# Router logits from the graphs' first rows on the vector engine, and expert choice on all partitions

## The chip, the cores and the metric

The kernel runs on one core of one Trainium2 chip. The metric is the device time of one execution in microseconds (us). Before the change it is 1921.93 us, the median of three runs (1921.78 to 1924.34).

## The reference

128 graphs of 128 nodes, each node with 1024 features, go through two blocks, each added to its input. `adj` has ones at about 3% of its places.

```python
def reference(x, adj, L0_gnn_W, L0_gnn_a, L0_ffn_router_w, L0_ffn_lora_down, L0_ffn_lora_up):
    x = x + gnn(layernorm(x), adj, W, a)
    x = x + ffn(layernorm(x), router_w, lora_down, lora_up)
    return x

def gnn(h, adj, W, a):                      # 16 heads of 64 features
    Wh = (h @ W) split into heads
    e = leaky_relu(Wh @ a[:, :, :F] + Wh @ a[:, :, F:], 0.2)
    att = softmax(where(adj == 0, -9e15, e)) * adj
    return elu(att @ Wh)

def ffn(x, router_w, lora_down, lora_up):   # 8 experts of rank 16, 2 chosen per graph
    logits = einsum('bh,eh->be', x[:, 0, :], router_w)
    gates = softmax over the 2 largest logits, 0 elsewhere
    down = einsum('blh,erh->bler', x, lora_down)
    return x + einsum('bler,ehr,be->blh', down, lora_up, gates)
```

So the router looks only at the first row (node 0) of each graph, and chooses two experts for the whole graph.

## The kernel before, in words

**Tiling.** The kernel works in passes over pairs of graphs (q = 0 to 63, then two more passes that finish the last group). Four graphs make a group g, so a group has an even pass and an odd one. Activations stand with the 128 nodes on the partitions; for products over the features it also has transposed copies. The matrix product with W is done per pair by seven products of blocks instead of eight (`project`, a Strassen-like scheme): each is eight fp32 products of 128x128 by 260 columns, which the profile records as 16. They are named by what they read: xt, or the sums s that GpSimd forms in `pair_sums`. A bank is a two-bank PSUM tile; three names x, y, z share two slots, so a product can start only when DVE or ACT has read the bank that it takes. Product 7 and product 4 share one accumulation, with a DVE read (L426) after each.

**Order.** The engines' order is written out by hand: the loop at the end of the kernel builds eight lists of tasks, `gaps[0]` to `gaps[7]`, runs the tasks of one list, then one of the seven products (in the order 1, 6, 2, 5, 7, 3, 4), then the next list. The order in which the tasks are called is the order on each engine, and each engine works strictly in this order. SP and ACT issue most transfers; on them a transfer that waits for something holds up all that stands behind it.

**One pair.** Pass q projects pair q, and in the same pass the pair before it (graphs i and i+1) is attended (`attend`, ph, L535), updated (`update`: hp L545, exp on ACT, xn L553 and L554) and measured (`second_stats`). `turn` then splits xn into 16-bit halves on ACT (L585) and transposes it by DMA (tt, L587), `rejoin` (y_t, L591) puts the halves together on ACT, and `join` (L607) forms y in place. `high` (L487, ACT) and `low` (L491, DVE) write the projected values in two parts for the next `attend`. Blocks 0 and 1 of the parts belong to the pair's first graph, 2 and 3 to its second.

**The feed-forward block of group g.** In the even pass (q = 2g + 2), in gap 6 between product 3 and product 4, `logits` multiplies column 0 of each graph's y_t by the router on PE: eight products of 4-column weights, with 8 moving columns (L615, 16 records), and one that brings the four graphs' rstd of row 0 onto four partitions (L618). `choose` takes on DVE the two largest logits of each graph, on 4 partitions: a `max` of eight values and then the position of each. In front of the last product of the same pass ACT computes exp of the difference (`ratio`). In the odd pass, gap 0, `fetch` spreads the chosen experts to all partitions by one product (pb, L683), forms row addresses on DVE (L686 to L693), and GpSimd gathers the experts' rows (eight transfers for down, L696, and one for up, L700). `weigh` forms the two gates on 4 partitions, and SP writes them to device memory and reads them back, one per partition (L654, L661). `ffn_down` (pd, L710, gap 4) needs the gathered rows and y_t; `ffn_up` (pu, L726) and DVE (L730) finish the group, and SP stores it.

**The last group** can't hide its gathers, so it multiplies with all experts (`down_dense`, `gates_dense`, `up_dense`), with expert tables loaded into W's place. `gates_dense` brings the gates onto the partitions by one more product (pg, L772).

**Once.** `experts` (L286) takes the mean out of the router and of the down tables, with partial sums on PE (`table_parts`, L280), and writes the down table to device memory for the gathers.

The functions and the lines of the order that matter here:

Of the kernel before, what the change touches and what calls it, by code (L numbers as in the profile page):

```python
# [8 lines left out]
F32 = mybir.dt.float32  # L9
F32R = mybir.dt.float32r  # L10
I32 = mybir.dt.int32
U32 = mybir.dt.uint32
# [13 lines left out]
def adj_ffn_kernel(  # L26
# [9 lines left out]
    a_t: bass.AP,  # L36
    down_t: bass.AP,
# [6 lines left out]
    P = 128  # L44
# [5 lines left out]
    E = router_t.shape[2]  # L50
# [7 lines left out]
    NG, _, G, _ = adj.shape  # L58
    QC = HALF // 2
# [20 lines left out]
    table = dram.tile([E * P, KC * R], F32, name="table")  # L80

# [54 lines left out]
    router_sb = const.tile([P, KC, E], F32, name="router_sb")  # L136
    down_sb = work.tile([P, G * TOP, R, KC], F32, tag="down", name="down_sb", bufs=1)

    def load_experts():
        nc.sync.dma_start(router_sb, router_t)  # L140
        nc.sync.dma_start(down_sb, down_t)
# [14 lines left out]
    ones_r = const.tile([P, P], F32R, name="ones_r")  # L156
    nc.vector.tensor_scalar(ones_r, mean_of, float(D), None, op0=ALU.mult)
    spread = const.tile([P, G, TOP], F32R, name="spread")
    nc.vector.memset(spread.bitcast(F32), 0.0)

    order = const.tile([G, E], F32, name="order")
    for e in range(E):
        nc.vector.memset(order[:, e:e + 1], float(E - e))

# [115 lines left out]
    def table_parts():  # L280
        return fourths([router_sb[:, k] for k in range(KC)],
                       [down_sb.rearrange("p e r k -> p k (e r)")[:, k] for k in range(KC)])

    slot = down_row = up_row = None

    def experts(part):  # L286

        nonlocal slot, down_row, up_row
        pr = ps_m.tile([P, HALF], F32, tag="pm", name="pr")
        nc.tensor.matmul(pr[:, 0:E + ER], sum_of, part, start=True, stop=True)  # L290
        for t, lo, n in ((router_sb.rearrange("p k e -> p e k"), 0, E),
                         (down_sb.rearrange("p e r k -> p (e r) k"), E, ER)):
            nc.vector.tensor_tensor(t, t, pr[:, lo:lo + n, None].to_broadcast([P, n, KC]),
                                    ALU.subtract)
        nc.sync.dma_start(table.rearrange("(e p) c -> p e c", p=P),
                          down_sb.rearrange("p e r k -> p e (r k)"))

        slot = const.tile([P, G * TOP], F32, name="slot")
        nc.vector.tensor_reduce(slot, ident.rearrange("p (j r) -> p j r", r=R), AX.X, ALU.add)
# [195 lines left out]
    def attention_weights(q):  # L495
# [8 lines left out]
        e = small.tile(shape, F32, tag="e", name="e")  # L504
# [6 lines left out]
        m = small.tile(shape, F32, tag="m", name="m")  # L511
        nc.vector.tensor_tensor(m, e, neg, ALU.max)
        p = small.tile([P, 2, 2, H], F32, tag="p", name="p")
# [4 lines left out]
        z = small.tile([P, 2, 2, H], F32, tag="z", name="z")  # L518
        nc.vector.tensor_mul(z, p, st["n"][:, :, pair, None].to_broadcast(z.shape))
        den = small.tile(shape, F32, tag="den", name="den")  # L520
# [88 lines left out]

    def logits(g):  # L610

        st = GRP[g]
        pl = ps_m.tile([P, HALF], F32, tag="pm", name="pl")
        for k in range(KC):
            nc.tensor.matmul(pl[:G, 0:E], st["y_t"][:, k, 0:G * P:P], router_sb[:, k],  # L615
                             start=(k == 0), stop=(k == KC - 1))

        nc.tensor.matmul(pl[:G, E:E + 1], st["rstd"], ident[:, 0:1], start=True, stop=True)  # L618
        st["pl"] = pl

    def choose(g):

        st = GRP[g]
        both = small.tile([G, E + 1], F32, tag="lg", name="lg")
        nc.vector.tensor_copy(both, st["pl"][:G, 0:E + 1])
        lg, dev = both[:, 0:E], both[:, E:E + 1]
        top = small.tile([G, 8], F32, tag="top", name="top")
        nc.vector.max(out=top, in_=lg)

        val = small.tile([G, 2, TOP], F32, tag="val", name="val")  # L630
        first = small.tile([G, E], F32, tag="first", name="first")
        mark = small.tile([G, 2, E], F32, tag="mark", name="mark")
        for s in range(TOP):
            nc.vector.scalar_tensor_tensor(mark[:, s], lg, top[:, s:s + 1], order,
                                           op0=ALU.is_equal, op1=ALU.mult)
            if s:
                nc.vector.tensor_scalar(first, order, val[:, 0, 0:1], None, op0=ALU.is_equal)
                nc.vector.scalar_tensor_tensor(mark[:, s], first, float(-E), mark[:, s],
                                               op0=ALU.mult, op1=ALU.add)
            nc.vector.tensor_reduce(val[:, 0, s:s + 1], mark[:, s], AX.X, ALU.max)  # L640
        if g < NG - 1:

            nc.vector.tensor_tensor(spread[0:G], ident[:G, :G, None].to_broadcast([G, G, TOP]),
                                    val[:, None, 0].to_broadcast([G, G, TOP]), ALU.mult)
        pr = small.tile([G, 2], F32, tag="pr", name="pr")
        nc.vector.tensor_sub(pr[:, 0:1], top[:, 1:2], top[:, 0:1])
        st.update(val=val, pr=pr, dev=dev)

    def put_away(val, name):

        own = small.tile([G, TOP, R], F32, tag="own", name="own", bufs=2)
        nc.vector.tensor_copy(own, val[:, :, None].to_broadcast([G, TOP, R]))
        rows = dram.tile([P, 1], F32, tag=name, name=name, bufs=2)
        nc.sync.dma_start(rows.rearrange("(g r) o -> g (r o)", g=G),  # L654
                          own.rearrange("g s r -> g (s r)"))
        return rows

    def of_rows(rows, name):

        mine = small.tile([P, 1], F32, tag=name, name=name)  # L660
        nc.sync.dma_start(mine, rows)  # L661
        return mine

    def ratio(g):
        st = GRP[g]
        nc.scalar.activation(st["pr"][:, 1:2], st["pr"][:, 0:1], AF.Exp, scale=st["dev"])

    def weigh(g):

        st = GRP[g]  # L670
        gate, pr = st["val"][:, 1], st["pr"]
        nc.vector.tensor_scalar(gate[:, 0:1], pr[:, 1:2], 1.0, None, op0=ALU.add)
        nc.vector.reciprocal(gate[:, 0:1], gate[:, 0:1])
        nc.vector.tensor_mul(gate[:, 1:2], pr[:, 1:2], gate[:, 0:1])
        if g < NG - 1:
            st["gate"] = of_rows(put_away(gate, "gates"), "gate")

    def fetch(g):

        st = GRP[g]  # L680
        pb = ps_m.tile([P, HALF], F32, tag="pm", name="pb")
        every = pb[:, 0:G * TOP]
        nc.tensor.matmul(every, ones_r, spread.rearrange("p g s -> p (g s)"), start=True,  # L683
                         stop=True)
        own = small.tile([P, G * TOP], F32, tag="own_slot", name="own_slot", bufs=1)
        nc.vector.tensor_tensor(own, every, slot, ALU.mult)  # L686
        mine = small.tile([P, 1], F32, tag="of_slot", name="of_slot", bufs=1)
        nc.vector.tensor_reduce(mine, own, AX.X, ALU.add)
        at_down = small.tile([P, G * TOP], U32, tag="at_down", name="at_down")
        nc.vector.tensor_scalar(at_down, every, float(-P), down_row, op0=ALU.mult,  # L690
                                op1=ALU.add)
        at_up = small.tile([P, 1], U32, tag="at_up", name="at_up")
        nc.vector.tensor_scalar(at_up, mine, float(-R), up_row, op0=ALU.mult, op1=ALU.add)  # L693
# [46 lines left out]
    down_all = block[1][:, 0:D].rearrange("p (k e r) -> p k e r", e=E, r=R)  # L740

    def load_all():
        nc.sync.dma_start(down_of_rows.rearrange("p e r k -> p e (r k)"),
                          table.rearrange("(e p) c -> p e c", p=P))
        nc.sync.dma_start(up_all, up_t)

# [13 lines left out]
    def gates_dense(g):  # L760

        st = GRP[g]
        val = st["val"]
        chosen = small.tile([G, TOP, E], F32, tag="chosen", name="chosen", bufs=1)
        for s in range(TOP):
            nc.vector.tensor_scalar(chosen[:, s], order, val[:, 0, s:s + 1], val[:, 1, s:s + 1],
                                    op0=ALU.is_equal, op1=ALU.mult)
        rows = work.tile([G, E, R], F32, tag="hp", name="chosen_rows")
        nc.vector.tensor_tensor(rows, chosen[:, 0, :, None].to_broadcast([G, E, R]),
                                chosen[:, 1, :, None].to_broadcast([G, E, R]), ALU.add)  # L770
        pg = ps_m.tile([P, HALF], F32, tag="pm", name="pg")
        nc.tensor.matmul(pg[:, 0:G], rows.rearrange("g e r -> g (e r)"), ident[:G, :G],  # L772
                         start=True, stop=True)
        gate = small.tile([P, G], F32, tag="gate_all", name="gate_all", bufs=1)
        nc.vector.tensor_copy(gate, pg[:, 0:G])
# [62 lines left out]
    for q in range(NQ + 2):  # L838
# [5 lines left out]
        if ffn and not part:  # L844
            gaps[6] += [(logits, g), (choose, g)]
        if q < NQ:
            gaps[6] += [(high, q, 3), (high, q, 1)]
            gaps[7].append((high, q, 2))
# [4 lines left out]
        if 0 < q <= NQ:  # L853
# [13 lines left out]
            gaps[5] += [(join, i), (join, i + 1)]  # L867
        if q + 1 < NQ:
# [3 lines left out]
            if q:  # L872
                gaps[4].append((first_stats, 2 * q + 3))
# [82 lines left out]
```

## Time and profile before

| what | value |
|---|---|
| median of three runs | 1921.93 us |
| the profiled execution, its own time | 1922.47 us |
| its span, first to last instruction | 1920.7 us |
| TensorE (PE) busy | 1903.6 us, 99% |
| weight loads (PEld), beside PE | 1565.7 us, 82% |
| VectorE (DVE) busy | 1630.6 us, 85% |
| ScalarE (ACT) busy | 1088.3 us, 57% |
| GpSimd (POOL) busy | 832.2 us, 43% |
| mean granted TensorE clock | 0.996 |
| logits products L615 and L618 | 17.8 us and 6.0 us busy |
| pb product L683 | 11.2 us busy |

How to read it: a busy share is an average over the whole run. PE's records overlap (a weight load and the next product run under the last one), so the durations of short products add up to more than they cost; distances between starts are the safer measure. Idle time is given in brackets behind a row of the timeline, with what ended it. In the chain of work that ended last, each step goes back to what released it.

### The profile page before, as it was taken

How to read it: one execution, taken by the hardware profiler on the slowest of the kernel's cores; microseconds unless marked ns; L12 is line 12 of the kernel's file. 1: busy time of each engine (PE TensorE's matmuls, PEld its weight loads, DVE VectorE, ACT ScalarE, POOL GpSimd, SP SyncE). 2: the span in 40 equal slices, each digit the busy share in tenths (PEclk: the TensorE clock that was granted, in tenths of full speed). 3: DMA queues.
4: the chain of work that ended last, by engine and by line, in shares of the span. 5: the costliest groups of instructions: out<-in, count | busy, mean ns of one | idle time of the engine just before them, and what ended most of it. 6: DMA issues, size and time to landing. Idle time of an engine off the chain costs nothing.

```text
span 1920.7 us, 30166 instructions
## 1 busy us (share of the span) xinstructions
PE 1903.6 (99%) x11003; PEld 1565.7 (82%) x11003; DVE 1630.6 (85%) x3416; ACT 1088.3 (57%) x1060; POOL 832.2 (43%) x1135
## 2 busy tenths in 40 slices
PE   9999999999999999999999999999999999999997
PEld 6888888888888888888888888888888888888885
DVE  5888988888988888888889888888888888888886
ACT  2656556556556555565565565565565655655653
POOL 3245434355344455334454443553444553344540
PEclk9999999999999999999999999999999999999998
DMA  7565655665656656566656556556556565566562
GB/s 299 142 186 132 199 172 153 192 172 147 197 171 164 190 153 169 179 158 190 186 132 198 172 153 192 170 149 194 172 167 188 147 176 178 158 190 187 123 168 95
DMA packets 348666, 329.27 MB, mean 171 GB/s; under 512 B 279016, under 2 KB 281064, under 8 KB 348008
## 3 DMA queue, kind: packets, MB, share of 16 engines
q1 hardware_dynamic: 330792, 285.39, 50.9%
q0 software_dynamic: 17008, 40.91, 7.3%
q8 instruction: 87, 1.43, 0.3%
q10 hardware_dynamic: 720, 1.06, 0.2%
q14 instruction: 59, 0.48, 0.1%
HBM read 193.58 MB, written 67.65 MB: 136 GB/s over the span
## 4 chain that ended last, share of the span: by engine, by line
PE 91%; DVE 4%; ACT 2%; DMA 2%; issue 1%; POOL 0%; DVEq 0%; POOLq 0%; ACTq 0%
PE pw L418 77%; PE ph L535 6%; PE pu L726 3%; PE pd L710 3%; DMA tt<-halves 1%; PE pl L615 1%; ACT y_t L591 1%; DVE xn L554 1%; ACT halves L585 1%; DVE xn L553 1%; DVE hp L545 1%; DVE stats L315 1%; PE pu L787 0%; DMA down<-table,at_down 0%; PE idle L149 0%
## 5 line engine op out<-in xcount | busy, mean ns | idle before, releaser
L418 PE MATMUL pw<-w_sb,xt 128*128 128x260 f32 (+1 forms) x4080 | 939.2, 385 | 0.0
L418 PEld LDWEIGHTS pw<-w_sb,xt 128*128 128x128 f32 x4080 | 764.4, 190 | 144.9 <-issue 24.9
L418 PE MATMUL pw<-w_sb,s 128*128 128x260 f32 (+1 forms) x3072 | 709.6, 384 | 1.9 <-DVE u L426 1.9
L418 PEld LDWEIGHTS pw<-w_sb,s 128*128 128x128 f32 x3072 | 581.9, 190 | 117.4 <-POOL xt L371 22.8
L319 POOL TENSOR_SCALAR rstd<-mv 128x2 f32<-128x2 f32 x126 | 27.4, 218 | 824.8 <-DVE mv L316 819.6
L591 ACT COPY y_t<-tt 128x2048 uint16<-128x2048 uint16 x126 | 315.1, 2510 | 76.1 <-DMA tt<-halves 75.8
L696 POOL DMA_INDIRECT down<-table,at_down x248 | 251.5, 1014 | 163.4 <-DVE e L509 89.8
L585 ACT COPY halves<-xn 128x2048 uint16<-128x2048 uint16 x126 | 239.3, 1899 | 145.0 <-DVE xn L554 145.0
L315 DVE BATCH_NORM_STATS2 stats<-xn 128x6 f32<-128x512 f32 x504 | 319.0, 675 | 0.1
L487 ACT ACTIVATE parts<-wh,rstd 128x512 fp32r<-128x512 f32 x192 | 133.8, 716 | 203.8 <-DVE wh L426 203.7
L552 ACT ACTIVATE ex<-hp 128x1024 f32<-128x1024 f32 x128 | 135.3, 1057 | 189.8 <-DVE hp L545 189.8
L730 DVE SCALAR_TENSOR_TENSOR xn<-pu,rstd,xn 128x512 f32<-128x512 f32 x248 | 169.0, 745 | 21.8 <-PE pu L726 21.8
L545 DVE TENSOR_TENSOR hp<-ph,att 128x512 f32<-128x512 f32 x256 | 161.1, 670 | 10.0 <-PE ph L535 9.7
L554 DVE SCALAR_TENSOR_TENSOR xn<-ex,xn 128x1024 f32<-128x1024 f32 x128 | 156.8, 1225 | 14.3 <-DVE xn L553 0.9
L535 PE MATMUL ph<-parts,adj_f 128*128 128x512 f32 x512 | 164.4, 442 | 1.3 <-ACT parts L487 0.8
L553 DVE SCALAR_TENSOR_TENSOR xn<-hp,xn 128x1024 f32<-128x1024 f32 x128 | 156.8, 1225 | 4.4
L607 ACT ACTIVATE xn<-xn,off,mul 128x1024 f32<-128x1024 f32 x128 | 151.3, 1231 | 1.5 <-POOL off L572 1.5
L426 DVE TENSOR_TENSOR wh<-pw,u 128x520 f32<-128x520 f32 (+1 forms) x128 | 89.2, 697 | 71.6 <-PE pw L418 62.6
L491 DVE SCALAR_TENSOR_TENSOR parts<-wh,rstd,parts 128x512 fp32r<-128x512 f32 x192 | 138.0, 746 | 11.3 <-ACT parts L487 11.3
L426 DVE TENSOR_TENSOR wh<-pw,p 128x520 f32<-128x520 f32 (+1 forms) x64 | 44.8, 700 | 81.9 <-PE pw L418 81.9
L535 PEld LDWEIGHTS ph<-parts,adj_f 128*128 128x128 f32 x512 | 96.6, 189 | 20.8 <-ACT parts L487 1.2
L320 POOL TENSOR_TENSOR rstd<-rstd,half_pow 128x2 f32<-128x2 f32 x126 | 89.7, 712 | 10.5
(154 smaller groups left out, 1448.3 us busy)
## 6 DMA issues: line engine op xcount, KB each, us to landing
xn<-in_x SPq DMA_DIRECT2D x128, 512.0 KB
xt<-in_x_t SPq DMA_DIRECT2D x127, 512.0 KB
out_y<-xn SPq DMA_DIRECT2D x124, 512.0 KB
adj_f<-in_adj_t POOLq DMA_DIRECT2D x32, 256.0 KB, 3.1
adj_i<-in_adj SPq DMA_DIRECT2D x32, 256.0 KB
down<-table,at_down POOLq DMA_INDIRECT x248, 4.1
w_sb<-in_w SPq DMA_DIRECT2D x3, 1040.0 KB
wt_sb<-in_w_t SPq DMA_DIRECT2D x1, 2048.0 KB
```

The source lines that it names most:

```text
L315: nc.vector.bn_stats(st[:, h, :], X[i][:, h * HALF:(h + 1) * HALF])
L418: nc.tensor.matmul(dst[:, j, cols], lhs[:, k, :], w_sb[:, rhs, k, j, cols], start=(first and k == 0), stop=(k == KH - 1), skip_group_check ...
L491: nc.vector.scalar_tensor_tensor(in_two(PARTS[q][:, 1, b]), block, rstd, in_two(PARTS[q][:, 0, b].bitcast(F32)), op0=ALU.mult, op1=ALU.sub ...
L535: nc.tensor.matmul(PH[i][h], GRP[g]["adj_f"][:, t, :], PARTS[q][:, s, NH * (i % 2) + h], start=(s == 0), stop=(s == 1))
L545: nc.vector.tensor_tensor(hp[:, h * HALF:(h + 1) * HALF].rearrange("p (h f) -> p h f", f=F), ph.rearrange("p (h f) -> p h f", f=F), att[:, ...
L553: nc.vector.scalar_tensor_tensor(xt, hp, 0.0, xt, op0=ALU.max, op1=ALU.add)
L554: nc.vector.scalar_tensor_tensor(xt, ex, 1.0, xt, op0=ALU.min, op1=ALU.add)
L585: nc.scalar.copy(halves, X[i].bitcast(U16).rearrange("p (d s) -> p s d", s=2))
L591: nc.scalar.copy(y_of(i).bitcast(U16).rearrange("p k (n s) -> p s k n", s=2), TT.pop(i).rearrange("p (s k) n -> p s k n", s=2))
L607: nc.scalar.activation(X[i], X[i], AF.Identity, bias=GRP[g]["off"][:, t:t + 1], scale=GRP[g]["mul"][:, t:t + 1])
L696: nc.gpsimd.indirect_dma_start(out=st["down"][:, j * R:(j + 1) * R].rearrange("p r k -> p (r k)"), out_offset=None, in_=table, in_offset=b ...
L730: nc.vector.scalar_tensor_tensor(y[:, cols], pu[t], st["rstd"][:, t:t + 1], y[:, cols], op0=ALU.mult, op1=ALU.add)
```

## The change

- The router no longer stands transposed on PE's side. `router_sb` now holds 32 features of each expert per partition: partition p belongs to graph p // 32 of the group and to features 32 (p % 32) onwards. A second copy `router_k`, with features as in y_t, goes to device memory for the last group.
- After `update`, SP writes row 0 of each graph to device memory (`first_row`, 4 KB each), and ACT reads the four rows of a group back as 128 partitions of 32 features (`spread_rows`). This read is issued in gap 3 of the even pass, on ACT behind the second `turn` and ahead of the two `rejoin`.
- `row_devs` (GpSimd, gap 3) and `row_parts` (DVE, gap 4) form a tile of 128 x 36: for each partition the partial logits of its own graph, in this graph's columns, and the rstd of row 0 alone in the last four.
- `logits` is one product of a 128x128 tile of ones with this tile. So every partition has the logits of all four graphs.
- `choose`, `weigh` and the addresses of `fetch` are done on all 128 partitions for four graphs at once, with a multiply by `slot` (own graph and slot of each partition) to pick a partition's own. The product pb, the write and read of the gates through device memory, and the product pg of the last group are gone.
- `fetch` moves from gap 0 of the odd pass to gap 6 of the even pass, right behind `choose`.
- The last group takes its partial logits from y_t and `router_k`.

```diff
-        pr = ps_m.tile([P, HALF], F32, tag="pm", name="pr")
-        nc.tensor.matmul(pr[:, 0:E + ER], sum_of, part, start=True, stop=True)
...
+        nc.tensor.matmul(pr[:, 0:ER], sum_of, part, start=True, stop=True)
+        nc.tensor.matmul(pr[:, ER:ER + E], mean_of, sums, start=True, stop=True)
...
+    def first_row(i):
+        g, t = divmod(i, G)
+        if t == 0:
+            GRP[g]["rows"] = dram.tile([G, D], F32, tag="rows", name="rows", bufs=2)
+        nc.sync.dma_start(GRP[g]["rows"][t:t + 1], X[i][0:1])
+
+    def spread_rows(g):
+        st = GRP[g]
+        st["row"] = small.tile([P, RD], F32, tag="first_row", name="first_row", bufs=2)
+        nc.scalar.dma_start(st["row"], st["rows"].rearrange("g (c d) -> (g c) d", d=RD))
+
+    def row_devs(g):
+        st = GRP[g]
+        st["add"] = small.tile([P, G * E + G], F32, tag="add", name="add", bufs=1)
+        nc.gpsimd.tensor_scalar(st["add"][:, G * E:], st["rstd"], ident[:, 0:1], None,
+                                op0=ALU.mult)
+
+    def row_parts(g):
+        st = GRP[g]
+        add = st["add"][:, 0:G * E].rearrange("p (g e) -> p g e", g=G)
+        if g < NG - 1:
+            prod = work.tile([P, E, RD], F32, tag="hp", name="prod")
+            nc.vector.tensor_tensor(prod, router_sb, st["row"][:, None].to_broadcast([P, E, RD]),
+                                    ALU.mult)
+            part = small.tile([P, E], F32, tag="part", name="part", bufs=1)
+            nc.vector.tensor_reduce(part, prod, AX.X, ALU.add)
+            nc.vector.tensor_tensor(add, of_graph[:, :, None].to_broadcast([P, G, E]),
+                                    part[:, None].to_broadcast([P, G, E]), ALU.mult)
+        else:
...
     def logits(g):
         st = GRP[g]
-        pl = ps_m.tile([P, HALF], F32, tag="pm", name="pl")
-        for k in range(KC):
-            nc.tensor.matmul(pl[:G, 0:E], st["y_t"][:, k, 0:G * P:P], router_sb[:, k],
-                             start=(k == 0), stop=(k == KC - 1))
-        nc.tensor.matmul(pl[:G, E:E + 1], st["rstd"], ident[:, 0:1], start=True, stop=True)
+        st["pl"] = ps_m.tile([P, HALF], F32, tag="pm", name="pl")
+        nc.tensor.matmul(st["pl"][:, 0:G * E + G], ones, st["add"], start=True, stop=True)
...
     def choose(g):
+        nc.vector.tensor_copy(both, st["pl"][:, 0:G * E + G])
...
         for s in range(TOP):
             if s:
+                nc.vector.tensor_tensor(mark, by_order,
+                                        val[:, 0, :, 0:1].to_broadcast(shape), ALU.is_equal)
+                nc.vector.scalar_tensor_tensor(lg, mark, NO_ENTRY, lg, op0=ALU.mult, op1=ALU.add)
+            nc.vector.tensor_reduce(top[:, s], lg, AX.X, ALU.max)
+            nc.vector.tensor_tensor(mark, lg, top[:, s, :, None].to_broadcast(shape), ALU.is_equal)
+            nc.vector.tensor_tensor(mark, mark, by_order, ALU.mult)
+            nc.vector.tensor_reduce(val[:, 0, :, s], mark, AX.X, ALU.max)
+        pr = small.tile([P, 2, G], F32, tag="pr", name="pr", bufs=2)
+        nc.vector.tensor_tensor(pr[:, 0], top[:, 1], top[:, 0], ALU.subtract)
+        nc.vector.tensor_tensor(pr[:, 0], pr[:, 0], dev, ALU.mult)
...
+    def own(val, name):
+        mine = small.tile([P, G * TOP], F32, tag="own", name="own", bufs=2)
+        nc.vector.tensor_tensor(mine, val.rearrange("p g s -> p (g s)"), slot, ALU.mult)
+        got = small.tile([P, 1], F32, tag=name, name=name)
+        nc.vector.tensor_reduce(got, mine, AX.X, ALU.add)
+        return got
...
     def weigh(g):
         if g < NG - 1:
-            st["gate"] = of_rows(put_away(gate, "gates"), "gate")
+            st["gate"] = own(gate, "gate")
...
     def fetch(g):
-        nc.tensor.matmul(every, ones_r, spread.rearrange("p g s -> p (g s)"), start=True,
-                         stop=True)
+        chosen = st["val"][:, 0]
...
         if ffn and not part:
             gaps[6] += [(logits, g), (choose, g)]
+            if g < NG - 1:
+                gaps[6].append((fetch, g))
...
+            if i < B - G:
+                gaps[1].append((first_row, i))
+                gaps[2].append((first_row, i + 1))
...
+        if ffn and not part:
+            if g < NG - 1:
+                gaps[3].append((spread_rows, g))
+            gaps[3].append((row_devs, g))
+            gaps[4].append((row_parts, g))
...
         elif ffn and part:
-            gaps[0].insert(0, (fetch, g))
             gaps[0].append((weigh, g))
```

## The prediction

> **What bounds the kernel now.** I read the page first: TensorE (PE) is busy 99% of the span, and in the chain that ended last nearly every step is PE's. So a change pays by the PE time that it takes out, as long as nothing new is late.
>
> ```profile
> PE 91%; DVE 4%; ACT 2%; DMA 2%; issue 1%; POOL 0%; DVEq 0%; POOLq 0%; ACTq 0%
> ```
>
> Next PE's timeline over one group of four graphs (its even pass; a group has two passes and takes 58.29 us, 215.77 to 274.06 from logits to logits).
>
> ```profile
> 208.66 3.67 PE L418 MATMUL pw<-w_sb,xt 128*128 128x260 f32 x16
> 212.17 3.67 PE L418 MATMUL pw<-w_sb,s 128*128 128x260 f32 x16
> 215.77 0.55 PE L615 MATMUL pl<-router_sb,y_t 128*4 128x8 f32 x16
> 216.18 0.19 PE L618 MATMUL pl<-ident,rstd 128*4 128x1 f32 x2
> 216.30 3.77 PE L418 MATMUL pw<-w_sb,xt 128*128 128x260 f32 x16
> 219.72 0.36 PE L683 MATMUL pb<-spread,ones_r 128*128 128x8 f32 x1
> 219.94 3.75 PE L418 MATMUL pw<-w_sb,xt 128*128 128x260 f32 x16
> 223.34 1.29 PE L535 MATMUL ph<-parts,adj_f 128*128 128x512 f32 x4
> 224.46 3.67 PE L418 MATMUL pw<-w_sb,s 128*128 128x260 f32 x16
> 227.77 1.28 PE L535 MATMUL ph<-parts,adj_f 128*128 128x512 f32 x4
> ```
>
> Columns: start, duration, instruction. Durations overlap in the pipeline, so I price by distances between starts. A product followed by a product takes 3.51 (208.66 to 212.17), one followed by ph takes 3.31 (224.46 to 227.77). From 212.17 to 223.34 there are three products: 3.51 + 3.51 + 3.31 = 10.33, and it took 11.17. The rest, **0.84 us a group**, is pl and pb, the instructions that the change takes away.
>
> Then DVE, ACT and SP in the same stretch, for what the new work must fit into:
>
> ```profile
> 212.37 0.70 DVE L426 TENSOR_TENSOR wh<-pw,u 128x520 f32<-128x520 f32 x1
> 215.88 0.70 DVE L426 TENSOR_TENSOR wh<-pw,p 128x520 f32<-128x520 f32 x1 [1.55 <-PE pw L418]
> 241.73 0.70 DVE L426 TENSOR_TENSOR wh<-pw,u 128x520 f32<-128x520 f32 x1 [2.06 <-PE pw L418]
> ```
>
> ```profile
> 206.84 1.90 ACT L585 COPY halves<-xn 128x2048 uint16<-128x2048 uint16 x1 [0.68 <-DVE xn L554]
> 208.65 2.49 ACT L591 COPY y_t<-tt 128x2048 uint16<-128x2048 uint16 x1
> 213.07 2.52 ACT L591 COPY y_t<-tt 128x2048 uint16<-128x2048 uint16 x1 [1.93 <-DMA tt<-halves]
> ```
>
> ```profile
> 224.63 0.28 SPq L654 DMA_DIRECT2D gates<-own  x1
> 228.25 0.33 SPq L661 DMA_DIRECT2D gate<-gates  x1
> ```
>
> Brackets are idle time and what ended it. DVE waits for PE 1.55 and 2.06 us here; ACT has 1.93 us ahead of the second y_t. SP's pair is a trip through device memory as the new one will be: the second issue waits 228.25 - 224.91 = 3.34 us for the first to land.
>
> **PE: removed 0.84, added about 0.28.** The new logits are one fp32 product with 128x128 ones, 36 moving columns, two records. The near row is turn_scores, four records of 128x128 weights and 16 columns:
>
> ```profile
> 46.70 0.51 PE L276 MATMUL ps<-fold,part 128*128 128x16 f32 x4
> 47.07 3.75 PE L418 MATMUL pw<-w_sb,xt 128*128 128x260 f32 x16
> 50.47 1.28 PE L535 MATMUL ph<-parts,adj_f 128*128 128x512 f32 x4
> ```
>
> 0.37 for four is 0.093 each, and the product behind takes 3.40 instead of 3.31: 0.09 once. Two records: 2 x 0.093 + 0.09 = 0.28. Ends: 0.24 (L290's two records of 136 columns start 0.24 before the next product) and 0.31 (pb's one record cost 0.22, plus 0.093). Gain 0.84 - 0.28 = 0.56 a group (0.53 to 0.60); the 31 groups before the last give **17.4 us** (16.4 to 18.6).
>
> A rule speaks against this. The Trainium skill ("TensorE: Matmul & The Clock Gate", section "LDWEIGHTS (loading the stationary operand)") says that a weight load takes its columns divided by 1.2, in ns. By loads alone the old logits cost 18 x 3.3 = 60 ns, pb 107, the new product 2 x 107 = 214: 0.05 us worse a group, 1.5 us slower in all. The row decides: sixteen records of 4-column weights start over 0.41 us, 26 ns each, so each pays for being an instruction, and the turns before and behind them cost as well. I take the rows.
>
> **Logits no longer wait for y_t.** L615 waits for the second y_t (ends at 215.59). Even passes, from ph to ph, are 27.24 in most groups, but 28.26 in the first, 28.04 in the last of the 31, and 0.09 to 0.21 longer in four others: 2.5 us together. Now only the transpose through DMA and y_t feed ffn_down, 20 us later. I count 2.5 (0 if the new inputs are as late there, which is the lower end).
>
> **fetch moves ahead**, from the next pass to right behind choose, without pb. On DVE its four operations (220.72 to 221.33, 0.6 us) now stand before two L491, product 4's read and the attention weights; on POOL the gathers stay behind the adjacency load, and what follows them there starts at 236.38. They begin about 1.5 us earlier, which ends the one wait of pd for down: **0.6 us**.
>
> **DVE, before the logits: row_parts.** 128x256 multiply, between the 0.28 us of 128x128 and the 0.67 of 128x512: 0.41. Its reduction, between 0.29 and 0.69: 0.42. A 128x32 operation: 0.19. With the gaps 1.1 us, at 212.30 ahead of the read at 212.37; the 1.55 us idle at 215.88 covers it, 0.45 left. Without that cover, a late read of product 3 would still only hold a PSUM bank that PE wants at 219.94.
>
> **DVE, behind the logits.** choose was ten operations from 216.50 to 218.17, 1.67. Now 13 on 128 partitions: copy 0.2, then twelve at 0.22 start to start (as 221.83 to 222.05 in the attention weights), 2.84. weigh has five operations for four, 0.2. Added 1.4. Idle up to and with 241.73: 0.30 + 0.23 + 2.06 = 2.6, of which PE's earlier arrival takes 0.56. 0.6 us is left, so DVE meets PE again at 241.73. On the way attend needs blocks 0 and 1 at 223.34; they were ready at 219.9 and will be at 221.4. If this cover is gone, product 7's bank is free late, but product 4 wants it only at 247.5.
>
> **The new trip of the first rows.** SP issues four more DMAs a group, each before a transpose that waits for the same X and an ACT copy of 1.9 us more, so none delays a transpose; the two gate DMAs go. The last row is final at 206.81 (xn L554). ACT issues the second leg behind halves (208.74) and before the first y_t, waiting for the landing; behind it on ACT stand both y_t, join and the parts. DVE's row_parts waits for the second leg, and behind it stand product 7's read, the group's adjacency, and all that follows. Price of the two landings: the skill ("DMA: Bandwidth & Descriptors", "Anatomy of one DMA") gives about 2.0 us fixed per DMA, mostly the receipt of the write. By it: 206.85 + 0.27 + 2.0 = 209.1, ACT's issue 0.33, + 2.0 = 211.5: before 212.30, no wait. By rows, 3.34 (gates) and 3.1 (adj_f, median to landing): 210.5 + 0.33 + 3.1 = 213.9, DVE stalls 1.6. The gates row had 2 MB of loads in flight (share of the DMA engines 1.0 from 223 to 227); from 207 to 209 the share is 0.00, so I lean to 212 to 213. At 213.9 too PE loses nothing: add is done at 215.0 for a logits product at 215.67, and product 7's read at 215.65 for product 4 at 215.95. ACT's wait, at most 2.1 us, is met by its 1.93 idle.
>
> **POOL** gets row_devs, 0.2 us before pair_sums; the first of those sums to be used is wanted by PE 14 us later: nothing.
>
> **Ends.** In the tail the chain is rstd on POOL, choose, exp, gates, dn. row_devs stands behind mul and off (0.9 us later), choose 1.3 longer; but exp waited for ACT's join until 1904.72 anyway, and the product pg with its two waits (1905.97 to 1907.08) goes. My sum has dn start at 1907.4 instead of 1907.12: 0.3 lost (-0.5 to +1). The start has sixteen short pc records less, one more product: nothing.
>
> **Sum.** 17.4 + 2.5 + 0.6 - 0.3 = 20.2. The profiled execution took 1922.47 (span 1920.7), 0.5 above the median: **1902.3 us**, 1.05% faster. The kernel's measurement tells about 0.2% from no change.
>
> **Rivals.**
> Partly eaten (1911): DVE's operations cost 0.3 instead of 0.22, and it lags into PE's bank waits, about 0.3 us a group, 9 us. Against it: the 0.6 us left and slack of over 2 us at each bank. For it: DVE goes from 85% to about 89%. 0.09.
> Cheaper than I say (1899): the two records hide in the turn between products, 0.18 instead of 0.28: 3 us. 0.10.
> Nothing (1921): PE is busy by the model, but the group's length is set by another loop, such as xn, transposes and buffers. Against it: passes without pl and pb differ by just these instructions. 0.04.
> Slower: the rows' trip. From a landing after 214.2 PE waits one for one, since product 4 needs the bank that DVE reads behind row_parts; at 214.8 the gain of 0.56 is gone. With two landings of 4.1, as the gathers' median: 206.85 + 0.27 + 4.1 + 0.33 + 4.1 = 215.65, PE loses 1.45 - 0.56 = 0.89 a group, 27.6 us: 1950. 0.05.
> The forecast's own case has 0.72: 1899.5 (0.60 a group, tail shorter) to 1906 (0.53, y_t waits not regained).
>
> Range 1899 to 1910: it leaves out most of the two last rivals and half of the first. Faster by over 0.2%: 0.91, within: 0.04, slower: 0.05.
>
> **What would show it.** Even passes from ph to ph of 26.7 instead of 27.24, odd ones unchanged at 31.05; the new logits followed 0.2 to 0.3 later by product 4; no PE wait at it; DVE's wait before row_parts under 1.6 us, and still some idle at 241.73's place. Wrong would be PE idle ahead of the logits or of product 4, or odd passes that grow.

## The result, and the profile after

| what | before | after |
|---|---|---|
| median of four runs each | 1922.91 us (1921.78 to 1924.34) | 1900.37 us (1899.30 to 1902.51) |
| the profiled execution, its own time | 1922.47 us | 1899.44 us |
| its span | 1920.7 us | 1897.3 us |
| PE busy | 99% | 1880.0 us, 99% |
| DVE busy | 85% | 1714.8 us, 90% |

The ratio is 0.9884 (95%: 0.9867 to 0.9901): 22.5 us or 1.16% faster, where 1902.3 us was forecast, with a range from 1899 to 1910. The chain that ended last is still PE's, with 95% instead of 91:

```profile
PE 95%; DVE 3%; DMA 1%; POOL 0%; issue 0%; SPq 0%; POOLq 0%; DVEq 0%; ACT 0%
```

PE's timeline over the same group as in the prediction:

```profile
208.45 3.67 PE L443 MATMUL pw<-w_sb,s 128*128 128x260 f32 x16
211.96 0.31 PE L683 MATMUL pl<-add,ones 128*128 128x36 f32 x2
212.10 7.26 PE L443 MATMUL pw<-w_sb,xt 128*128 128x260 f32 x32
219.00 1.29 PE L560 MATMUL ph<-parts,adj_f 128*128 128x512 f32 x4
```

Product 3 starts at 208.45 and ph at 219.00, 10.55 us for three products that take 10.33 undisturbed. So the new logits cost 0.22, where pl and pb had cost 0.84. No bracket stands on any of the lines: PE waits for nothing here.

DVE in the same group, with the second new operation and the rest of choose left out:

```profile
208.48 0.38 DVE L663 TENSOR_TENSOR prod<-router_sb,first_row 128x256 f32<-128x256 f32 x1
...
209.35 0.69 DVE L667 TENSOR_TENSOR add<-of_graph,part 128x32 f32<-128x32 f32 x1
209.96 0.68 DVE L451 TENSOR_TENSOR wh<-pw,u 128x520 f32<-128x520 f32 x1
...
212.16 0.70 DVE L451 TENSOR_TENSOR wh<-pw,p 128x520 f32<-128x520 f32 x1
...
237.40 0.70 DVE L451 TENSOR_TENSOR wh<-pw,u 128x520 f32<-128x520 f32 x1 [0.33 <-PE pw L443]
```

L663 carries no wait: the first rows were there in time. The read at 212.16 had 1.55 us of idle before it in the kernel before and has none now; 237.40 is the place of 241.73, with 0.33 us of idle left of 2.06.

The trip of the rows, from ACT's timeline and then from SP's:

```profile
203.11 1.90 ACT L610 COPY halves<-xn 128x2048 uint16<-128x2048 uint16 x1 [0.67 <-DVE xn L579]
204.38 0.33 ACTq L646 DMA_DIRECT2D first_row<-rows  x1
```

```profile
203.10 0.24 SPq L640 DMA_DIRECT2D rows<-xn  x1
```

SP's last issue ends at 203.34 and ACT's, which waits for the landing, starts at 204.38: 1.04 us. GpSimd, the second of its pair sums (it matters below) and the first gather of the experts' rows:

```profile
208.61 1.38 POOL L394 TENSOR_TENSOR s<-s,xt 128x512 f32<-128x512 f32 x1
...
216.19 1.06 POOL L745 DMA_INDIRECT down<-table,at_down  x1 [0.69 <-DVE of_slot L716]
```

The gather stands 4.23 us behind the logits (216.19 - 211.96); before the change it was 5.73 in this group (215.77 to 221.50), and 6.03 to 6.04 in 26 of the 31. Last, PE in the tail, where it waits for the last group's row_devs and for dn:

```profile
1880.31 0.64 PE L683 MATMUL pl<-add,ones 128*128 128x36 f32 x2 [2.90 <-POOL add L653]
...
1885.92 7.13 PE L833 MATMUL pu<-w_sb,dn_all 128*128 128x512 f32 x16 [1.41 <-DVE dn_all L823]
```

**Where the 23.4 us of the span came from**, by the lengths of the passes from the first ph of one to the first ph of the next:

| part | before | after | gain |
|---|---|---|---|
| even passes, sum (31) | 846.8 | 825.8 | 21.0 |
| of it the medians, 31 x (27.24 - 26.63) | | | 18.9 |
| of it what single passes exceed the median | 2.4 | 0.3 | 2.1 |
| odd passes, sum | 960.4 | 960.3 | 0.1 |
| start to the first ph | 50.47 | 48.66 | 1.8 |
| the pass ahead of the first group | 28.0 | 28.1 | -0.1 |
| tail, from the last ph | 35.0 | 34.4 | 0.6 |

The 1.8 at the start are none of the change's: in the execution before, the granted clock was 0.50 to 0.54 from 30 to 33 us and one product took 5.41 there instead of 3.72, behind a gap of PE of 1.86 us that the execution after has too (1.85). In the nine variants of the changed kernel below the first ph comes at 49.2 to 51.9. In the tail dn_all comes 0.86 later behind the last ph (22.29 instead of 21.43), and the dense product pu takes 1.42 less (7.13 instead of 8.55) at a higher granted clock. So some 3.2 of the 23.4 are the clock at the two ends, and about 20.2 are the change's.

### The profile page after: what moved, and what is told of

It reads as the page before. It is cut to its first block, busy times and chain, and to the rows that moved or that the text cites. A ratio compares the mean times of both kernels' runs of the same rounds, so it can differ in the third digit from the quotient of the medians.

```text
span 1897.3 us, 29572 instructions
## 1 busy us (share of the span) xinstructions
PE 1880.0 (99%) x10444; PEld 1553.1 (82%) x10444; DVE 1714.8 (90%) x3642; ACT 1084.3 (57%) x1060; POOL 833.8 (44%) x1167
## 4 chain that ended last, share of the span: by engine, by line
PE 95%; DVE 3%; DMA 1%; POOL 0%; issue 0%; SPq 0%; POOLq 0%; DVEq 0%; ACT 0%
PE pw L443 82%; PE ph L560 6%; PE pu L775 3%; PE pd L759 3%; DMA w_sb<-in_w 1%; DVE stats L340 0%; PE pu L833 0%; POOL down L745 0%; PE pl L683 0%; DVE w_sb L841 0%; DMA down<-table,at_down 0%; DVE parts L516 0%; DVE hp L570 0%; DVE xn L578 0%; PE rows L231 0%
## 5 line engine op out<-in xcount | busy, mean ns | idle before, releaser
L745 POOL DMA_INDIRECT down<-table,at_down x248 | 258.9, 1044 | 90.6 <-issue 64.9
L393 POOL TENSOR_TENSOR s<-xt 128x512 f32<-128x512 f32 x64 | 81.7, 1277 | 17.6 <-DMA xt<-in_x_t 17.6
```

The lines of the kernel that those rows point to most:

```text
L745: nc.gpsimd.indirect_dma_start(out=st["down"][:, j * R:(j + 1) * R].rearrange("p r k -> p (r k)"), out_offset=None, in_=table, in_offset=b ...
```

## The experiments

All differences below are against the changed kernel (passes of 26.63 and 31.06, 1900.37 us) unless the kernel before is named. Its medians beside these runs were 1922.92 and 1923.59, and its single run beside the four kernels from reads_y_t to three_hops took 1922.71. Where a kernel has a single run, I go by its passes.

**Is the old logits' price in instructions or in loaded columns?** The kernel before, with one of the eight feature blocks in the logits (it leaves out the other seven, so other experts are chosen):

```diff
-        for k in range(KC):
+        for k in (KC - 1,):
             nc.tensor.matmul(pl[:G, 0:E], st["y_t"][:, k, 0:G * P:P], router_sb[:, k],
-                             start=(k == 0), stop=(k == KC - 1))
+                             start=True, stop=True)
```

> The kernel before, with one of the eight logits products (its y_t column times one chunk of the router; the logits are then those of the last 128 features alone, so other experts are chosen). The wait for y_t stays. My theory, each short product pays for being an instruction: 14 records less at 26 ns is 0.36 us a group, even passes 26.88 instead of 27.24, 11 us faster in all. Rival, the weight loads by their columns (3.3 ns for four): 0.05 us a group, 1.5 us in all, passes 27.19.

Measured: 1912.77, ratio to before 0.9943 (0.9923 to 0.9963); even passes 26.89, odd ones 31.06. The even pass lost 0.35 us for 14 records, 25 ns each. The load times by columns would have given 46 ns for all 14 together, so they are not what such a record costs; 25 ns is, whatever in it takes them. The waits for y_t stayed, as this product still reads y_t: the even passes sum to 838.1, 4.5 over 31 medians, and in six of them PE stands idle for y_t ahead of the logits, about 4 us in all. One odd pass took 32.47, as ffn_down waited for gathered rows there.

**What does one 128-column record cost?** The new product doubled:

```diff
         nc.tensor.matmul(st["pl"][:, 0:G * E + G], ones, st["add"], start=True, stop=True)
+        nc.tensor.matmul(st["pl"][:, 0:G * E + G], ones, st["add"], start=True, stop=True)
```

> The changed kernel with its product of ones done twice into the same place (same values). By turn_scores, 0.093 us a record: two records more are 0.19 us a group, even passes 26.82 instead of 26.63, 5.8 us slower. If the first product hides in the turn between products and only its records' 36 columns count (0.03 us each), 0.06 a group and 1.9 us. By the load rule, 107 ns each: 0.21 a group.

Measured: 1907.38 (0.9917 of before, 0.9897 to 0.9937), 7.0 more; even passes 26.85. Two records cost 0.22, 0.11 each. So the first pair, at 0.22, has nothing for a turn, and for full-width weights the rule's columns divided by 1.2 (107 ns) is met.

**Was pb worth 0.22?** One product of ones, in fp32r, 8 columns wide, back in the odd pass (called ahead of the rest of gap 0; the tile of ones is made as fp32r for it, with the same values):

```diff
+    def once_more(g):
+        pb = ps_m.tile([P, HALF], F32, tag="pm", name="pb")
+        nc.tensor.matmul(pb[:, 0:G * TOP], ones_r, ones_r[:, 0:G * TOP], start=True, stop=True)
```

> The changed kernel with a product like the removed pb (fp32r, 128x128 ones, 8 columns) put back where pb stood, its result unused; no DVE work and no wait with it. My price of pb, 0.22 us a group: passes from ph to ph 26.85 instead of 26.63, 6.8 us slower. Rival: pb cost only its load, 0.11, and pl the rest of the 0.84: 3.4 us slower.

Measured: 1904.55 (0.9901 of before, 0.988 to 0.9921), 4.2 more, and the pass with it 26.75, 0.12 longer. pb was worth 0.12, not 0.22, and so pl 0.72 of the 0.84. The distance from pb to the next product is 0.22 here too, but the product ahead of pb takes 3.40 instead of 3.51: counting from one start alone put 0.1 of pl's price on pb.

**What did moving fetch bring?** It goes back to gap 0 of the odd pass:

```diff
-            if g < NG - 1:
-                gaps[6].append((fetch, g))
...
+            gaps[0].insert(0, (fetch, g))
             gaps[0].append((weigh, g))
```

> The changed kernel with fetch back at the head of the odd pass. My theory: the gathers start some 1.5 us later and PE still meets them at pd only in rare groups, so all regular passes stay at 26.63 and 31.06 and the waits of pd for down are 0.5 to 2 us in all. Rival: the earlier gathers are part of the gain, and odd passes grow by several tenths.

Measured, one run: 1915.77, and my theory fell. The even passes stay 26.63, but the odd ones have a median of 31.51 instead of 31.06; their sum is 974.2 instead of 960.3, 13.9 us more. GpSimd's first and last gather for ffn_down in a group, then PE's ffn_down:

```profile
222.56 1.06 POOL L745 DMA_INDIRECT down<-table,at_down  x1 [2.33 <-DVE of_slot L716]
...
232.49 0.95 POOL L745 DMA_INDIRECT down<-table,at_down  x1 [0.30 <-issue]
```

```profile
236.40 0.45 PE L759 MATMUL pd<-y_t,down 128*32 128x128 f32 x6
237.08 1.94 PE L759 MATMUL pd<-y_t,down 128*32 128x128 f32 x58 [0.23 <-DMA down<-table,at_down]
```

Six records of pd run, those of three graphs. It goes on at 237.08, when the rows of the fourth, which the last two gathers bring, are there. GpSimd is done with the last of these gathers (233.44) 2.96 us before pd starts; in most groups of the kernel before it is 3.98, and in the changed kernel 5.05. Two things make up the 1.01 lost against the kernel before. From the first gather to pd there are 13.84 us instead of 14.19, as PE comes 0.61 earlier and choose takes longer: 0.35. And the eight gathers take GpSimd 10.87 instead of 10.21: 0.66. The first alone costs nothing: in five of the 31 groups the gathers take 9.8 to 10.0 at the same 13.84, pd does not wait, and the pass stays at 31.06. Why the gathers take longer in the other 26 stays open. So PE's gain alone does not make the gathers late, but with the longer gathers it does, and the move of fetch by 1.65 us (5.88 to 4.23 behind the logits) covers it.

**What were the waits for y_t worth?** A small product that must wait for y_t goes ahead of the logits, and as a control the same one with the identity as its weights:

```diff
+        if g < NG - 1:
+            nc.tensor.matmul(st["pl"][:G, 64:64 + E], st["y_t"][:, KC - 1, 0:G * P:P],
+                             ones[:, 0:E], start=True, stop=True)
```

```diff
+            nc.tensor.matmul(st["pl"][:G, 64:64 + E], ident[:, 0:P:P // G],
+                             ones[:, 0:E], start=True, stop=True)
```

> The changed kernel with one small product ahead of the product of ones in all groups but the last: weights are four columns of y_t as in the logits before, 8 moving columns of ones, into unused columns of the same bank. It brings back PE's wait for y_t. Its own two records and turns are priced by reads_ident beside it. My theory: passes in which y_t is late come back, 2.5 us in all over reads_ident, most of it in few groups. Rival: the 2.5 us of before were not y_t; then the two kernels are equal.

> The control of reads_y_t: the same small product with four columns of the identity as weights, which are always ready. Two records of 26 ns and a turn of about 0.1 on both sides: 0.05 to 0.25 us a group, even passes 26.7 to 26.9, all equal.

Measured, one run each: 1914.82 and 1915.28; even passes 26.96 in both, summing to 837.1 and 836.0. The sum of the one that reads y_t is 1.1 us longer, and 1.0 of it lies in the first group (28.25 against 27.25). The late passes that the kernel before had in groups further on did not come back. They were y_t's all the same: in the trace of before PE stands idle ahead of the logits until y_t in five even passes (0.91, 0.10, 0.15, 0.10 and 0.73), 2.0 us of the 2.4. In this run y_t is in time in all groups but the first, and why it was not so before stays open.

The control told more, and against what I expected: two records of 4-column weights cost 0.33, more than two with 128 columns (0.22). The weight loads of the control, then those of the changed kernel, show where it lies:

```profile
99.95 0.09 PEld L684 LDWEIGHTS pl<-ones,ident 128*4 128x4 f32 x2 [0.34 <-issue]
```

```profile
211.74 0.41 PEld L683 LDWEIGHTS pl<-add,ones 128*128 128x128 f32 x2
```

The wide load starts at 211.74, 0.22 before its product at 211.96, under the last record of product 3. The narrow one starts with its product (99.95), after 0.34 us in which the load path stood, though it waited for no data. The same 0.34 stands in all groups of the control, and ahead of the old logits in the kernel before. It is not the few columns alone: in the changed kernel it also stands ahead of the weights of ffn_down, which have 32 columns, and of ffn_up, which have 128 columns but 32 rows:

```profile
231.67 1.74 PEld L759 LDWEIGHTS pd<-y_t,down 128*32 128x32 f32 x64 [0.34 <-issue]
237.29 0.31 PEld L775 LDWEIGHTS pu<-up,dn 32*128 32x128 f32 x8 [0.34 <-issue]
```

So turning from 128x128 weights to smaller ones has a toll here. With 26 ns a record it is 0.33 - 0.05 = 0.28 for the 4-column weights. By that the old pl comes to 18 x 0.026 + 0.28 = 0.75, near the 0.72 measured.

**How much room has the rows' trip?** One or three more copies through device memory, issued by ACT, ahead of the last leg (`range(3)` for the second kernel):

```diff
+        for hop in range(1):
+            moved = dram.tile([G, D], F32, tag="moved%d" % hop, name="moved", bufs=2)
+            nc.scalar.dma_start(moved, st["rows"])
+            st["rows"] = moved
```

> The changed kernel with the four rows copied once more inside device memory, by ACT, before they are spread: one landing and one issue (0.33) more. In the changed kernel row_parts starts at 208.48 with its data long there, and PE suffers only when it starts after about 209.95 (product 4 needs the bank that DVE reads behind it, at 212.10). The first leg took about 1.0 from issue to ACT's next issue. My theory: the second leg lands about 1.4 to 2.4 later than now, near 208, DVE waits at most 1 us, passes stay at 26.63. Rival: landings of 3 to 4 us, as the gates' row had, and passes grow by 1 to 2 us.

> As one_hop with three copies in a row. Each adds 1.4 to 2.4 us, so the data lands between 210 and 214 on the clock of the group that starts its product of ones at 211.96. My theory: what lies behind about 209.95 is lost one for one, 0 to 4 us a group, with PE idle ahead of the product of ones or of product 4 put down to DVE; if row_parts starts at t, the loss is t - 209.95 within 0.3. Rival: slack elsewhere takes it up and PE loses less than half of that; or ACT, which is held up before both y_t, is what PE waits for.

Measured, one run each. One hop: 1906.73; even passes 26.63 at the median (sum 828.2), though DVE now waits 1.05 us for the rows in a typical group, 33 us in all. PE feels it in two groups alone (28.05 and 27.82), where it waits for add. The odd passes grew by 2.3 in their sum, which I had not expected. The gathers start 1.3 later than in the changed kernel (5.55 behind the logits in most groups), but it is not the shortage seen with fetch back, as pd waits in no group. From pd to the product behind it there are 1.98 us instead of 1.92, and in some groups 0.2 more; the profile names nothing that PE waits for there, and the cause stays open.

Three hops: 2026.8, even passes 30.92, odd 31.06. DVE's and PE's timelines in one group, with granted clocks below:

```profile
225.17 0.43 DVE L667 TENSOR_TENSOR prod<-router_sb,first_row 128x256 f32<-128x256 f32 x1 [4.51 <-DMA first_row<-moved]
...
226.09 0.19 DVE L671 TENSOR_TENSOR add<-of_graph,part 128x32 f32<-128x32 f32 x1
```

```profile
220.54 3.67 PE L443 MATMUL pw<-w_sb,s 128*128 128x260 f32 x16
226.42 0.38 PE L687 MATMUL pl<-add,ones 128*128 128x36 f32 x2 [2.21 <-DVE add L671]
226.94 8.93 PE L443 MATMUL pw<-w_sb,xt 128*128 128x260 f32 x32
235.52 1.28 PE L560 MATMUL ph<-parts,adj_f 128*128 128x512 f32 x4
```

Undisturbed, the logits would start at 220.54 + 3.51 = 224.05, product 4 at 224.19, and DVE could begin up to 222.04 without holding PE. DVE's work with the rows began 3.13 after that, and product 4 is 2.75 late: one for one, less about 0.4, just outside the 0.3 expected, mostly since DVE's 128x32 operation took 0.19 instead of 0.69. So the slower rival's mechanism and its point of decision are right. Its price is not: from product 4 to ph it takes 8.58 where 6.90 is usual. The windows of the profile (each from one time to another, with its length, then PE, PEld, DVE, ACT, POOL, then the granted clock, DMA share and GB/s) tell why; the last is from a group further on:

```profile
226.00:227.00 1.00, 0.44 (x3) 0.36 (x3) 0.96 (x4) 1.00 (x2) 0.00 (x0) 0.95 0.00 0
227.00:228.00 1.00, 1.00 (x3) 0.81 (x4) 0.97 (x3) 1.00 (x1) 0.00 (x0) 0.50 0.07 16
...
665.00:666.00 1.00, 1.00 (x6) 0.85 (x6) 1.00 (x2) 1.00 (x1) 0.33 (x2) 1.00 0.11 41
```

After 2.2 us without PE work the clock falls to 0.50 and stays so until 230.3, and the group pays 1.68 us more. The Trainium skill ("TensorE: Matmul & The Clock Gate", "HAM oscillation — how this bites in real kernels") names gaps above about 3.4 us for this; here 2.2 us were enough, but not always. In 23 of the 31 groups the clock fell, after gaps of 1.90 to 2.43 (3.55 in the first group); in eight it did not, after gaps of 1.99 to 2.24 (2.04 ahead of 664), and their passes are 29.2 to 29.4. The trace's clock record suggests what decides. The low stretches last 3.41 us, in three groups 6.83, and they begin on a raster of 3.413 us: at 165.46, 226.90 and 353.19, for instance, 18 and 37 steps apart. In the eight groups the gap began 1.44 to 1.70 us behind a step of this raster, in the 23 others 0.01 to 1.39. So it went by the place of the gap on the raster and not by its length alone; no run here moves the gap on purpose.

**Why does the 128x32 operation take 0.69 instead of 0.19?** The third operation of row_parts as a copy, with one input in SBUF (it leaves out the mask, so all four graphs share the sum of their logits and other experts are chosen):

```diff
-            nc.vector.tensor_tensor(add, of_graph[:, :, None].to_broadcast([P, G, E]),
-                                    part[:, None].to_broadcast([P, G, E]), ALU.mult)
+            nc.vector.tensor_copy(add, part[:, None].to_broadcast([P, G, E]))
```

> The changed kernel in which the third operation of row_parts copies each partition's partial logits to all four graphs' columns instead of multiplying them by the graph's mask (the logits are then sums over the four graphs, and other experts are chosen): one SBUF input instead of two. In the changed kernel this operation took 0.69 us in all 31 groups, where 128x32 operations take 0.19 elsewhere, and it ends as GpSimd's second pair sum ends. My theory: it waits for GpSimd because both read two SBUF operands, and with one input it takes about 0.2. Rival: the broadcast of its operands makes it slow, and it stays near 0.7. The time stays within 1 us by both, since PE is not waiting for it.

Measured, one run: 1901.55, passes unchanged. The copy is as slow (DVE, then GpSimd):

```profile
211.44 0.68 DVE L667 COPY add<-part 128x32 f32<-128x32 f32 x1
```

```profile
210.69 1.39 POOL L394 TENSOR_TENSOR s<-s,xt 128x512 f32<-128x512 f32 x1
```

My theory of the two inputs is refuted, and so is the rival, the broadcast: with three hops the very same two-input operation took 0.19 in all 31 groups (line 226.09 above), when GpSimd was idle. The copy ends at 212.12, GpSimd's operation at 212.08, and in the changed kernel it is 210.04 and 209.99. In all 31 groups of both it ends 0.03 to 0.05 behind GpSimd's operation, and so it does with one hop, where DVE comes 1.3 us later. So it ends as GpSimd's operation ends. Not every GpSimd operation does this: the 128x32 operations of choose take 0.19 beside GpSimd's operation on two columns (213.04 to 213.76). The Trainium skill ("SBUF — State Buffer", "SBUF: two separate sides") says that DVE and GpSimd share a pair of ports, which one of them locks for a whole instruction, against DVE operations with two inputs in SBUF and those that use both ports for one; the durations here fit that, and no run here shows the ports themselves.

**A better version?** row_devs of the last group directly behind the rstd that it reads, ahead of mul and off:

```diff
             rstd_of(rstd, mv[:, :, 1])
-
+            if t == G - 1:
+                row_devs(g)
...
-            gaps[3].append((row_devs, g))
```

> The changed kernel with row_devs right behind the rstd on GpSimd, ahead of mul and off. In the last group PE waited 2.9 us for it; the three operations that it now passes take 0.65. My theory: that wait becomes 2.2 to 2.3, the tail shorter by 0.6 us, all passes unchanged; by time not to be told from the changed kernel. Rival: the wait ends with another input (row_parts ends 1.1 us before row_devs there), or join on ACT, which starts 0.3 later, takes its place: no gain.

Measured: median 1901.19 of four runs (1900.81 to 1904.62), 0.9888 of before (0.9867 to 0.991), passes unchanged. PE's wait for the last logits fell from 2.90 to 2.27, the 0.6 expected, but the time can't be told from the changed kernel's. None of these variants is measurably faster than the changed kernel.

## Why the prediction was right, step by step

- **The bound.** PE was the limit and stayed it, and its time fell by instructions taken out. Right: even passes of 26.63 for 26.7, odd ones 31.06 for 31.05.
- **PE, 0.56 a group.** Measured 0.61, so 18.9 for 17.4. The term off is the new product: 0.22 for 0.28. Its near row, turn_scores, was divided wrongly: the prediction shared 0.37 among four records and took the other 0.09 for a turn, paid once. All of it, 0.46 for four, is 0.115 a record and 0.23 for two, and ones_twice shows no turn. The split of the 0.84 was wrong (pb 0.12 for 0.22), which entered only the upper end of the price, 0.31.
- **The rule against it.** Columns divided by 1.2, taken as the price of a record, is right for the new product (0.11 a record) and was wrong for the old one by a factor of twelve (0.72 against 0.060): 26 ns a record and the toll of the turn. Choosing the rows was right, and ones_twice with one_of_eight show both halves.
- **y_t, 2.5.** The uneven even passes gave 2.1. In the trace of before 2.0 of their 2.4 are PE's idle time for y_t, so the term is right in kind. Putting the wait back brought 1.1, so the rest went because y_t itself was in time in that run, which the prediction did not foresee.
- **fetch, 0.6.** Against the kernel before the odd passes give 0.1: the last one became 0.97 us shorter, but one at group 11 became 0.91 longer, where pd waits for down. GpSimd starts that group's gathers 2.0 later than the others' (6.26 behind the logits instead of 4.24). The variants have that pass at 31.3 to 32.0, three_hops at 31.06; its cause stays open. What the step failed to see is that without the move 13.9 of the gain would have gone.
- **DVE.** Before the logits 1.48 us instead of 1.1, and 0.3 more for the nz behind (0.94, where it took 0.62 before and 0.42 in three_hops, with GpSimd idle): all 1.55 of the cover are used, and 0.45 were to be left. Behind the logits choose takes 2.67 instead of 2.84, and 0.33 of idle is left where 0.6 was forecast. The cover held, more narrowly than forecast.
- **The rows' trip.** No wait of DVE, as leaned to; the first leg was 1.04 us from the end of its issue, 0.99 to 1.11 in all groups, and not 3.34 as the gates'. The last leg took 3.0 in one_hop (208.86 to 211.86), near the 3.1 of the row. The 2.0 us that the prediction takes from the Trainium skill ("DMA: Bandwidth & Descriptors", "Anatomy of one DMA") are given there for transfers that GpSimd issues; these are SP's and ACT's, and neither leg took 2.0. The rival at 0.05 was a real mechanism: three_hops gave 2026.8.
- **Ends.** dn 0.86 later instead of 0.3. The other 3.2 us there are the clock of two single executions, which the sum could not know; without them the traces give 20.2, as forecast.

That agreement is partly luck: PE's term was 1.5 too small, y_t, fetch and tail together 1.5 too large.

## What to carry to other kernels

Where PE is the bound, price a small product by the distances between starts from the product ahead of it to the one behind it, and price the change of weight shape with it: two narrow records cost more here (0.33) than two full ones (0.22). When PE gets faster, look at what feeds it, and start that earlier where the order allows it: with the gathers left in their old place, 13.9 us of the gain were given back in one run. Take the duration of a small DVE operation with GpSimd's work of that moment beside it, not from a row where GpSimd is idle.

## What the runs showed of the hardware

- Two records with 4-column weights between 128-column products cost 0.33 us, two with 128 columns 0.22. The narrow load is not pulled ahead of its product: 0.34 us of idle on the load path, which also stands ahead of 128x32 and of 32x128 weights.
- A 128x32 DVE operation on SBUF took 0.19 us with GpSimd idle and 0.68 to 0.69 beside GpSimd's sums, with two inputs or one, ending 0.03 to 0.05 behind them.
- Gaps of about 2.2 us without PE work halved the granted clock for 3.41 us in 23 of 31 groups (6.83 in three of them), which cost 1.68 us in the group shown. In the eight others, with gaps as long, it stayed at 1.00.
- ACT issued a transfer at 204.38 in the middle of a copy that ran from 203.11 to 205.01. A wait of a transfer on ACT's queue can so lie under the operation ahead of it.
- A row written to device memory landed 1.04 us after its issue with the DMA engines empty (share 0.01), against 3.34 for the gates with loads in flight (share 1.0).
